# Self attention: projections of queries, keys and modulation without padding, spread to 32 rows a head through DRAM

## The chip, the cores and the metric

The kernel runs on one core of a Trainium2 chip. The core has five engines with their own instruction queues: TensorE (PE, matrix products into PSUM; its weight loads, PEld, overlap its products), VectorE (DVE), ScalarE (ACT), GpSimd (POOL) and SyncE (SP, which here issues most transfers between DRAM and the on-chip memory SBUF). Engines take their instructions in the order of their queues and wait for one another through semaphores. The transfers run on 16 DMA engines.

The metric is device time of one execution in microseconds (us), the median over runs. The profile is of one execution of its own; its times are made against that execution.

## The reference, cut to what matters

A post-norm decoder layer on 4 batches of 1,024 tokens and 256 features, all in 32-bit floats: self attention, cross attention with 154 context tokens, and a mixture of 8 experts, each followed by a layer norm. Only the first of the three concerns the change:

```python
q = (hidden_states @ Wq + bq).reshape(b, s, NH, HD).transpose(0, 2, 1, 3)
k = (hidden_states @ Wk + bk).reshape(b, s, NH, HD).transpose(0, 2, 1, 3)
v = (hidden_states @ Wv + bv).reshape(b, s, NH, HD).transpose(0, 2, 1, 3)
scores = jnp.einsum('bhqd,bhkd->bhqk', q, k) / jnp.sqrt(jnp.asarray(HD, q.dtype))
mod = jax.nn.sigmoid(hidden_states @ cg_W + cg_b + (cons_vec @ am_W + am_b))
scores = scores * mod.transpose(0, 2, 1)[..., None]
probs = jax.nn.softmax(scores, axis=-1)
ctx = jnp.einsum('bhqk,bhkd->bhqd', probs, v).transpose(0, 2, 1, 3).reshape(b, s, h)
causal_ctx = _mha(hidden_states, hidden_states, ca_Win, ca_bin, ca_Wout, ca_bout, CAUSAL_HEADS)
ctx = ctx * (1.0 - CAUSAL_W) + causal_ctx * CAUSAL_W
meta_ctx = _mha(ctx, ctx, mc_Win, mc_bin, mc_Wout, mc_bout, META_HEADS)
ctx = ctx * (1.0 - META_W) + meta_ctx * META_W
return ctx @ Wo + bo
```

There are NH = 16 heads of HD = 16 features. Each head and token has one modulation, a sigmoid, with which its scores are multiplied.

## The kernel before

**Layout of heads.** Queries and keys stand with features on the partitions and tokens along the row. A head has 16 features, but it is given 32 partitions, so that four heads (a group g of four, NG = 4) fill a tile of 128 partitions and each head lies on its own 32 rows of the PE array. Of the 32 rows, 16 are features, 15 are zero, and row 31 (MR) is special: in k it holds -1, in q it later takes the maximum of the token's scores. A product over all 32 rows is then the score less its maximum, which can go straight into the exponential.

The padding is made in the weights. load_head_cols (L141) loads a weight of 256 x 256 into a staging tile and copies its columns into a zeroed tile of 256 x 512, and load_head_bias (L153) does the same for a bias, with -1 in row 31 for k. cgw, the weight of the modulation, repeats each head's column 32 times.

**Projecting.** project (L283) multiplies 128 columns of such a weight with xT, the transposed tokens of the batch (256 x 1,024), into a PSUM tile "big" of 128 x 1,024; there are two of these tiles, shared with the score products. It is 4 products of 128 x 512, and each is two instructions in the profile, 8 in all. For each group there are three calls: project_mod (evacuated by ACT as a tanh, then scaled by POOL), project_q (evacuated by DVE, with the bias and the modulation) and project_k (evacuated by ACT with the bias). So a batch makes 12 calls. The tiles q and k come from a pool "qk" of 6, the modulation from a pool "ex" of 10.

**Maxima and exponentials.** For each group and each quarter (part) of 256 query tokens there are 8 units of each kind. A unit of maxima (L410) makes two score products (L422) into a "big" tile, and DVE takes the maximum over keys (L429); after 8 of them the maxima are transposed (L343) and added to row 31 of q (L346). A unit of exponentials (L441) makes the score products with all 32 rows (L460) and ACT exponentiates them (L471; L468 at the end of the batch); every four units a product with the values follows (L480).

**Order of a batch.** The loop over n (L829) runs 128 units of exponentials, 32 a group, with the maxima 12 units ahead (lead). In groups 0 to 2 it calls project_mod, project_q and project_k of the next group at units 4, 8 and 12 (project_at, L825). In group 3 it starts the causal attention instead. Then come two attentions of four heads each, the output product and the layer norm, the cross attention (L926 to L965), and, for the last norm of the batch, a generator that runs on into the next batch's loop ("behind").

begin(b) (L753) starts a batch: it transposes the tokens into xT, calls the three projections of group 0, makes the first 12 units of maxima and the values v16 and v64. For batch 0 it runs at once. For batches 1 to 3 it is a generator, and one step of it is taken at each step of the batch before, from its last output product on: two steps there, eight in the layer norm, and then one in each unit of the cross attention's loop, which has 36.

**Queues.** What an engine does is in the order of the program as the framework has placed it, and a wait in a queue holds all behind it. SP's queue at the start holds, in this order: the tokens of batch 0, the weights, the bias table and context of the cross attention, and a fill of the DRAM buffer scratch with zeros (L260, 9.2 MB in rows of 1 KB) and row numbers (L261, 9,216 pieces of 8 bytes), which the experts use at the end. After that SP issues four transfers a batch until the experts begin. POOL's queue at the start pads the weights and loads the biases.

Of the kernel before, what the change touches and what calls it, by code (L numbers as in the profile page):

```python
# [46 lines left out]
def decoder_layer(ctx: ExitStack, tc: tile.TileContext, a, out):  # L47
# [18 lines left out]
    def flat(t):  # L66
        return t.rearrange("p a b -> p (a b)")
# [65 lines left out]
    with tc.tile_pool(name="wA", bufs=1) as wA, tc.tile_pool(name="work", bufs=2) as work:  # L133


        def load_plain(name, src, n):
            t = wA.tile([P, src.shape[0] // P, n], F32, tag=name, name=name)
            nc.sync.dma_start(t, src.rearrange("(c p) n -> p c n", p=P))
            return t

        def load_head_cols(name, src):  # L141

            st = work.tile([P, NC2, H], F32, tag="ex", name="stage", bufs=EXB)
            nc.sync.dma_start(st, src.rearrange("(c p) n -> p c n", p=P))
# [8 lines left out]
        def load_head_bias(name, src, extra):  # L153

            t = wA.tile([P, NG], F32, tag=name, name=name)
            if extra == 0.0:
                nc.vector.memset(t, 0.0)
            else:
                tmp = work.tile([P, NG], F32, tag="tmpb", name="tmpb")
                nc.vector.memset(tmp, extra)  # L160
                nc.vector.tensor_scalar(t, tmp, rowmx, None, ALU.mult)
            v = src.rearrange("(g j d) -> j d g", j=4, d=HD)
            for j in range(4):
                nc.gpsimd.dma_start(t[32 * j : 32 * j + HD, :], v[j])
            return t

        def load_cols(name, src):
            t = wA.tile([P, src.shape[0] // P], F32, tag=name, name=name)
            nc.gpsimd.dma_start(t, src.rearrange("(c p) -> p c", p=P))
            return t  # L170
# [4 lines left out]
            return t  # L175


        idv = ident.rearrange("p (j w) -> p j w", w=32)
        rowmx = const.tile([P, 1], F32, name="rowmx")
        nc.vector.reduce_sum(rowmx, idv[:, :, MR], axis=AX.X)  # L180

        mxcol = []
        for i in range(2):
# [2 lines left out]
            mxcol.append(m)  # L186

        nc.sync.dma_start(gw, a["L0_ffn_gate_w"].rearrange("(c p) e -> p c e", p=P))
        wq = load_head_cols("wq", a["L0_attn_Wq"])
        bq = load_head_bias("bq", a["L0_attn_bq"], 0.0)  # L190

        cgs = work.tile([P, NC2, NH], F32, tag="cgs", name="cgs", bufs=1)
        nc.sync.dma_start(cgs, a["L0_attn_cg_W"].rearrange("(c p) h -> p c h", p=P))
        cgw = wA.tile([P, NC2, NH, 32], F32, tag="cgw", name="cgw")
        for c in range(NC2):
            nc.gpsimd.tensor_copy(cgw[:, c], cgs[:, c, :].unsqueeze(2).to_broadcast([P, NH, 32]))
# [5 lines left out]
        amr = work.tile([18, NH, 32], F32, tag="ex", name="amr", bufs=EXB)  # L202
        nc.vector.tensor_copy(amr, am.unsqueeze(2).to_broadcast([18, NH, 32]))
# [5 lines left out]
        cgb = wA.tile([P, NG], F32, tag="cgb", name="cgb")  # L209
        ps = small()  # L210
        for g in range(NG):
# [3 lines left out]
        nc.vector.tensor_scalar(cgb, ps[:, 0:NG], 0.5, None, ALU.mult)  # L215

        wk = load_head_cols("wk", a["L0_attn_Wk"])
        bk = load_head_bias("bk", a["L0_attn_bk"], -1.0)
        wv = load_plain("wv", a["L0_attn_Wv"], H)
        bv = load_bcast("bv", a["L0_attn_bv"])  # L220

# [17 lines left out]
        xbq = load_head_bias("xbq", a["L0_xattn_bq"], 0.0)  # L239
        xwk = load_head_cols("xwk", a["xWkT"])  # L240
        xbk = load_head_bias("xbk", a["L0_xattn_bk"], 0.0)
# [22 lines left out]
        def ex_tile(shape, name):  # L264
            return work.tile(shape, F32, tag="ex", name=name, bufs=EXB)
# [14 lines left out]
        def qk_tile(name):  # L280
            return work.tile([P, S], F32, tag="qk", name=name, bufs=6)

        def project(w, lo, xT):  # L283

            ps = big()
            for tb in range(2):
                for c in range(NC2):
                    nc.tensor.matmul(  # L288
                        ps[:, tb, :],
                        w[:, c, lo : lo + P],  # L290
                        xT[:, c, tb * 512 : (tb + 1) * 512],
                        start=(c == 0),
                        stop=(c == NC2 - 1),
                    )
            return ps
# [22 lines left out]
        class Clock:  # L318
# [62 lines left out]
        class Self:  # L381
# [4 lines left out]
                self.clock = Clock()  # L386
                self.st = [{} for _ in range(NG)]

            def project_mod(self, g):
                ms = project(cgw, g * P, self.xT)  # L390
                mod = ex_tile([P, S], "mod")
                nc.scalar.activation(
                    mod, flat(ms), AF.Tanh, bias=cgb[:, g : g + 1], scale=0.5
                )
                nc.gpsimd.tensor_scalar(mod, mod, 1.0, 0.5, ALU.add, ALU.mult)
                self.st[g]["mod"] = mod

            def project_q(self, g):
                q = self.st[g]["q"] = qk_tile("q")
                qs = project(wq, g * P, self.xT)  # L400
                nc.vector.scalar_tensor_tensor(
                    q, flat(qs), bq[:, g : g + 1], self.st[g]["mod"], ALU.add, ALU.mult
                )

            def project_k(self, g):
                k = self.st[g]["k"] = qk_tile("k")
                ks = project(wk, g * P, self.xT)
                nc.scalar.activation(k, flat(ks), AF.Identity, bias=bk[:, g : g + 1])

            def maxima(self, n):  # L410
                u, s = divmod(n, 8)
# [341 lines left out]
        def begin(b):  # L753

            y = ys[b]
            xT = work.tile([P, NC2, S], F32, tag="xT", name="xT", bufs=1)
            for c in range(NC2):
                transpose_tokens(xT, y, c)
                yield
            v16 = work.tile([P, NT, VP], F32, tag="v16", name="v16", bufs=1)  # L760
            nc.gpsimd.memset(v16, 1.0)
            sa = Self(xT, v16, None)
            for step in (sa.project_mod, sa.project_q, sa.project_k):
                step(0)
                yield
            add_bias(y, bo)
            v64 = work.tile([P, NT, H], F32, tag="v64", name="v64", bufs=1)
            begun[b] = sa, xT, v64
            vals = values(xT, wv, 0, bv, v16, NH, HD, 1)
            for n in range(lead):  # L770
                sa.maxima(n)
                next(vals, None)
                sa.clock.step()
                yield
            yield from values(xT, ca[0], 2 * H, ca[3], v64, MH, MD, 0)
# [36 lines left out]
        for b in range(B):  # L812
# [526 lines left out]
```

## Time and profile before

| What | Value |
|---|---|
| median of 3 runs | 3435.27 us (3431.95 to 3436.01) |
| the profiled execution | 3433.82 us |
| its span, first to last instruction | 3432.0 us |
| granted PE clock, mean | 0.976 |
| start, 0 to 80 us: PE busy, granted clock | 61.34 us, 0.74 |
| loop of batch 0, groups 0 to 2, 80 to 291 us: PE, DVE, ACT busy | 202.48, 130.87, 119.58 us |
| group 3 and the two attentions of four heads, 291 to 594 us: PE busy | 296.50 us |
| begin of batch 1 beside the layer norm, 594 to 620 us: PE, DVE busy | 26.00, 16.68 us |
| cross attention, 620 to 753 us: PE, DVE, ACT busy | 129.29, 73.01, 82.11 us |
| experts and end, 2773 to 3432 us: PE busy | 621.80 us |

A busy time is the time in which at least one instruction of that engine ran; matrix products overlap and their ends are modelled, so a busy PE need not be at its peak. A batch lasts 686 us: its context transfer is issued at 620.38, 1308.23 and 1994.39 us. In a line of the timeline the numbers are the start and the time taken; in a line of groups they are the number of instructions, the busy time, the mean of one in ns, and the engine's idle time before them with what ended it. PE here counts products and PEld weight loads.

### The profile page before, as it was taken

The page shows a single profiled execution, that of the slowest core. Times are in us where ns is not written, and L with a number is a line of the kernel's source. Part 1 is how long each engine was busy: PE and PEld are TensorE (multiplying, and loading weights), DVE is VectorE, ACT ScalarE, POOL GpSimd, SP SyncE. Part 2 cuts the span into 40 slices and gives each one's busy share as a digit, 9 for nine tenths or more (in the row PEclk, how much of TensorE's full clock was granted, in tenths as well). Part 3 has the DMA queues.
Part 4 walks back from the last instruction along what each step waited for, and adds up shares of the span by engine and source line. Part 5 has one row for each costly group of instructions (what it writes and reads, how often), then busy time and mean ns, then how long its engine had stood idle before and what let it go on. Part 6 is the DMA issues. An engine that isn't in the chain of part 4 may idle for free.

```text
span 3432.0 us, 60936 instructions
## 1 busy us (share of the span) xinstructions
PE 3300.5 (96%) x25260; PEld 2085.6 (61%) x25260; DVE 1725.3 (50%) x3571; ACT 1601.0 (47%) x3130; POOL 373.3 (11%) x601
## 2 busy tenths in 40 slices
PE   7999999999999999999999999999999999999997
PEld 4555667565556675665566756555667665555554
DVE  3565555565655555656555556565556551122224
ACT  1555534375555453755554537555534731222223
POOL 4000000000000000000000000000000018222123
PEclk7999999999999999999999999999999999999999
DMA  9000000000000000000000000000000052111114
GB/s 204 1 2 1 1 1 1 3 21 14 1 1 1 1 1 3 21 13 2 1 1 1 1 3 9 1 2 1 1 1 1 1 203 82 47 42 44 44 44 157
DMA packets 75866, 84.13 MB, mean 25 GB/s; under 512 B 15136, under 2 KB 65928, under 8 KB 75592
## 3 DMA queue, kind: packets, MB, share of 16 engines
q1 hardware_dynamic: 68040, 61.53, 6.4%
q0 software_dynamic: 7552, 18.70, 1.6%
q8 instruction: 202, 3.31, 0.4%
q14 instruction: 72, 0.59, 0.1%
HBM read 46.52 MB, written 33.69 MB: 23 GB/s over the span
## 4 chain that ended last, share of the span: by engine, by line
PE 85%; DVE 9%; ACT 2%; issue 2%; POOL 1%; DMA 1%; SPq 0%; ACTq 0%; DVEq 0%; POOLq 0%
PE big L288 10%; PE big L422 8%; PE big L530 8%; PE one L566 7%; PE acc L584 7%; PE big L1226 7%; PE one L480 7%; DVE mxp L429 6%; PE one L460 4%; PE acc L1248 4%; PE one L697 3%; PE big L1178 3%; PE big L662 3%; PE one L302 2%; PE acc L716 2%
## 5 line engine op out<-in xcount | busy, mean ns | idle before, releaser
L429 DVE TENSOR_REDUCE mxp<-big 128x2 f32<-128x1024 f32 x512 | 610.3, 1218 | 305.5 <-PE acc L460 252.1
L422 PE MATMUL big<-k,q 31*128 31x512 f32 x2048 | 595.8, 644 | 30.2 <-DVE mxp L429 26.6
L471 ACT ACTIVATE ex<-one 128x512 f32<-128x512 f32 x696 | 391.3, 601 | 247.4 <-PE acc L460 182.9
L460 PE MATMUL one<-q,k 32*128 32x256 f32 x2784 | 501.9, 397 | 0.0
L269 DVE CUSTOM_DVE_ANT_0 prob<-big,zero_t 128x1024 f32<-128x1024 f32 x256 | 303.6, 1222 | 271.9 <-PE big L530 271.7
L460 PEld LDWEIGHTS one<-q,k 32*128 32x128 f32 x2784 | 326.8, 186 | 31.0 <-ACT ex L471 2.5
L549 ACT ACTIVATE prob<-prob,nmx 128x1024 f32<-128x1024 f32 x256 | 293.0, 1153 | 20.2 <-DVE nmx L269 19.7
L530 PE MATMUL big<-mk,mq 64*128 64x512 f32 x1024 | 284.4, 633 | 2.5 <-ACT ex L468 2.5
L422 PEld LDWEIGHTS big<-k,q 31*128 31x128 f32 x2048 | 180.1, 189 | 171.5 <-DVE mxp L429 93.6
L571 ACT COPY pt<-one 128x512 f32<-128x512 f32 x256 | 137.8, 588 | 311.7 <-PE one L566 311.7
L566 PEld LDWEIGHTS one<-ident,prob 128*128 128x128 f32 x2048 | 221.8, 142 | 98.1 <-issue 92.4
L1226 PE MATMUL big<-wall,xt 128*128 x576 | 272.5, 596 | 1.8 <-POOL by L1202 1.8
L460 PE MATMUL acc<-q,k 32*128 32x256 f32 x928 | 263.9, 404 | 0.0
L566 PE MATMUL one<-ident,prob 128*128 128x128 f32 x2048 | 257.6, 279 | 0.0
L480 PE MATMUL one<-ex,v 128*32 128x256 f32 x4096 | 248.4, 382 | 0.0
L1236 DVE TENSOR_TENSOR hidr<-big,slr 128x512 f32<-128x512 f32 x72 | 49.8, 691 | 332.7 <-ACT slr L1234 332.7
L682 ACT ACTIVATE xs<-xs,xmx 128x154 f32<-128x154 f32 x512 | 174.4, 414 | 69.6 <-DVE xmx L269 69.6
L480 PEld LDWEIGHTS one<-ex,v 128*32 128x32 f32 x4096 | 119.8, 110 | 122.1 <-ACT ex L471 35.8
L573 DVE COPY pt<-one 128x512 f32<-128x512 f32 x256 | 164.3, 683 | 10.9 <-PE one L566 10.9
L269 DVE CUSTOM_DVE_ANT_0 xs<-big,bias 128x154 f32<-128x154 f32 x512 | 132.0, 314 | 66.0 <-ACT avx L724 33.5
L530 PEld LDWEIGHTS big<-mk,mq 64*128 64x128 f32 x1024 | 99.6, 191 | 101.7 <-issue 79.4
L460 PEld LDWEIGHTS acc<-q,k 32*128 32x128 f32 x928 | 155.4, 186 | 0.0
(266 smaller groups left out, 4715.2 us busy)
## 6 DMA issues: line engine op xcount, KB each, us to landing
xg<-scratch SPq DMA_DIRECT2D x72, 129.0 KB, 2.0
scratch<-empty SPq DMA_DIRECT2D x1, 9216.0 KB
r<-result SPq DMA_DIRECT2D x8, 1024.0 KB, 11.2
y<-in_x_dram SPq DMA_DIRECT2D x4, 1024.0 KB, 5.3
wall<-in_L_ffn_w_gate_dram SPq DMA_DIRECT2D x8, 512.0 KB, 10.3
wall<-in_L_ffn_w_up_dram SPq DMA_DIRECT2D x8, 512.0 KB, 10.8
wall<-in_L_ffn_w_down_dram SPq DMA_DIRECT2D x8, 512.0 KB, 11.6
bias<-in_fside_BxSxS_dram SPq DMA_DIRECT2D x4, 616.0 KB, 4.5
```

What stands on the lines that cost most here:

```text
L269: nc.vector.tensor_tensor_reduce(out=out, in0=ps, in1=bias, scale=-1.0, scalar=3.0e38, op0=ALU.add, op1=ALU.min, accum_out=low,)
L288: nc.tensor.matmul(ps[:, tb, :], w[:, c, lo : lo + P], xT[:, c, tb * 512 : (tb + 1) * 512], start=(c == 0), stop=(c == NC2 - 1),)
L422: nc.tensor.matmul(ps[:, jj, :], st["q"][r : r + MR, tok : tok + P], st["k"][r : r + MR, kb * 512 : (kb + 1) * 512], start=True, stop=True,)
L429: nc.vector.reduce_max(mxp[:, t, kb, 2 * pair : 2 * pair + 2], ps, axis=AX.X)
L460: nc.tensor.matmul(scs[jj][:, i * QW : (i + 1) * QW], st["k"][r : r + MR + 1, kc * P : (kc + 1) * P], st["q"][r : r + MR + 1, part * QW : ...
L471: nc.scalar.activation(ex[:, jj, :], scs[jj], AF.Exp, scale=1.0 / HD**0.5)
L480: nc.tensor.matmul(av[32 * j : 32 * j + 32, 0:QW], self.v[:, kc, h * VW : h * VW + 32], exs[kc // 2, j // 2][:, j % 2, i : i + QW], start= ...
L530: nc.tensor.matmul(pss[i][:, kb, :], q[r : r + MD, t * P : (t + 1) * P], k[r : r + MD, kb * 512 : (kb + 1) * 512], start=True, stop=True,)
L549: nc.scalar.activation(p, p, AF.Exp, bias=nmx[:, i : i + 1], scale=-1.0, accum_out=sm[:, t % 4, i : i + 1],)
L566: nc.tensor.transpose(ps[:, kc * P : (kc + 1) * P], probs[u][i][:, at : at + P], ident)
L584: nc.tensor.matmul(av[64 * i : 64 * i + 64, (t % 4) * P : (t % 4 + 1) * P], v[:, kc, h * MD : (h + 1) * MD], flipped[u][i][:, kc, :], star ...
L1226: nc.tensor.matmul(ps[:, g, :], xt[:, c * P : (c + 1) * P], wall[:, bass.ds(off + (g * NC2 + c) * D, D)], start=(c == 0), stop=(c == NC2 - 1),
```

## The change

The weights of queries, keys and modulation are no longer padded: wq and wk are loaded as they are (256 x 256), cgw repeats a head's column 16 times instead of 32, and the biases and cgb have 2 columns instead of 4. A projection of 128 columns now holds 8 heads, so all heads take two calls for each of the three (half 0 and half 1), 6 a batch instead of 12.

All six are made in begin. The evacuated tiles qh and kh hold 8 heads of 16 rows. Each is written to a DRAM buffer, q_rows or k_rows (512 rows of 1,024), with each head's 16 rows at the first 16 of its 32 (rows_of). The other 16 rows of each head are written once at the start from a tile pads: zeros for q, and zeros with -1 in the last row for k. A group's q and k are then loaded from 128 rows of these buffers (load): group 0's between the two halves in begin, the others' at unit 4 of the group before. All these transfers are issued by SP. Pads takes the place of xT in its pool of one tile. In begin three steps are added.

For padding, load_head_cols and load_head_bias stay in use for the cross attention alone. The scheduled order changes with it: at the start, SP's queue has the pads ahead of the weights, and the bias table and context behind the fill of scratch, where the writes and loads of batch 0's q and k follow.

```diff
+        pads = work.tile([P, 2, S], F32, tag="xT", name="pads", bufs=1)
+        nc.gpsimd.memset(pads[:, 0, :], 0.0)
+        idv = ident.rearrange("p (j w) -> p j w", w=HD)
+        last_of = const.tile([P, 1], F32, name="last_of")
+        nc.vector.reduce_sum(last_of, idv[:, :, HD - 1], axis=AX.X)
+        nc.vector.tensor_scalar(pads[:, 1, :], pads[:, 0, :], last_of, None, ALU.subtract)
+        qkd = [dram.tile([NG * P, S], F32, name=n) for n in ("q_rows", "k_rows")]
+
+        def rows_of(i, half, lo):
+
+            return qkd[i].rearrange("(t h w) s -> t h w s", t=NC2, w=32)[half, :, lo : lo + HD, :]
+
+        for i in range(2):
+            for half in range(NC2):
+                nc.sync.dma_start(rows_of(i, half, HD), pads[:, i, :])
...
-        wq = load_head_cols("wq", a["L0_attn_Wq"])
-        bq = load_head_bias("bq", a["L0_attn_bq"], 0.0)
+        wq = load_plain("wq", a["L0_attn_Wq"], H)
+        bq = load_cols("bq", a["L0_attn_bq"])
...
-        wk = load_head_cols("wk", a["L0_attn_Wk"])
-        bk = load_head_bias("bk", a["L0_attn_bk"], -1.0)
+        wk = load_plain("wk", a["L0_attn_Wk"], H)
+        bk = load_cols("bk", a["L0_attn_bk"])
...
-            def project_mod(self, g):
-                ms = project(cgw, g * P, self.xT)
+            def project(self, half):
+
+                ms = project(cgw, half * P, self.xT)
                 mod = ex_tile([P, S], "mod")
                 nc.scalar.activation(
-                    mod, flat(ms), AF.Tanh, bias=cgb[:, g : g + 1], scale=0.5
+                    mod, flat(ms), AF.Tanh, bias=cgb[:, half : half + 1], scale=0.5
                 )
                 nc.gpsimd.tensor_scalar(mod, mod, 1.0, 0.5, ALU.add, ALU.mult)
-                self.st[g]["mod"] = mod
-
-            def project_q(self, g):
-                q = self.st[g]["q"] = qk_tile("q")
-                qs = project(wq, g * P, self.xT)
+                yield
+                q = ex_tile([P, S], "qh")
+                qs = project(wq, half * P, self.xT)
                 nc.vector.scalar_tensor_tensor(
-                    q, flat(qs), bq[:, g : g + 1], self.st[g]["mod"], ALU.add, ALU.mult
+                    q, flat(qs), bq[:, half : half + 1], mod, ALU.add, ALU.mult
                 )
-
-            def project_k(self, g):
-                k = self.st[g]["k"] = qk_tile("k")
-                ks = project(wk, g * P, self.xT)
-                nc.scalar.activation(k, flat(ks), AF.Identity, bias=bk[:, g : g + 1])
+                nc.sync.dma_start(rows_of(0, half, 0), q)
+                yield
+                k = ex_tile([P, S], "kh")
+                ks = project(wk, half * P, self.xT)
+                nc.scalar.activation(k, flat(ks), AF.Identity, bias=bk[:, half : half + 1])
+                nc.sync.dma_start(rows_of(1, half, 0), k)
+                yield
+
+            def load(self, g):
+
+                for i, n in enumerate("qk"):
+                    t = self.st[g][n] = qk_tile(n)
+                    nc.sync.dma_start(t, qkd[i][g * P : (g + 1) * P, :])
...
-            for step in (sa.project_mod, sa.project_q, sa.project_k):
-                step(0)
-                yield
+            yield from sa.project(0)
+            sa.load(0)
+            yield from sa.project(1)
...
-            project_at = {4: sa.project_mod, 8: sa.project_q, 12: sa.project_k}
...
-                if g < 3 and s in project_at:
-                    project_at[s](g + 1)
+                if g < 3 and s == 4:
+                    sa.load(g + 1)
```

More of the change, by code (lines that the diff above doesn't have):

```diff
@@ L151, in load_head_cols, with load_head_bias @@
             return t.rearrange("p c h w -> p c (h w)")
-        def load_head_bias(name, src, extra):
+        def load_head_bias(name, src):
             t = wA.tile([P, NG], F32, tag=name, name=name)
[L156 to L161, printed above, removed]
+            nc.vector.memset(t, 0.0)
             v = src.rearrange("(g j d) -> j d g", j=4, d=HD)
@@ L175, in load_bcast @@
             return t
-        idv = ident.rearrange("p (j w) -> p j w", w=32)
-        rowmx = const.tile([P, 1], F32, name="rowmx")
-        nc.vector.reduce_sum(rowmx, idv[:, :, MR], axis=AX.X)
+        pads = work.tile([P, 2, S], F32, tag="xT", name="pads", bufs=1)
[10 more added lines that the diff above has]
+                nc.sync.dma_start(rows_of(i, half, HD), pads[:, i, :])
         mxcol = []
@@ L188, in decoder_layer @@
         nc.sync.dma_start(gw, a["L0_ffn_gate_w"].rearrange("(c p) e -> p c e", p=P))
-        wq = load_head_cols("wq", a["L0_attn_Wq"])
-        bq = load_head_bias("bq", a["L0_attn_bq"], 0.0)
+        wq = load_plain("wq", a["L0_attn_Wq"], H)
+        bq = load_cols("bq", a["L0_attn_bq"])
         cgs = work.tile([P, NC2, NH], F32, tag="cgs", name="cgs", bufs=1)
         nc.sync.dma_start(cgs, a["L0_attn_cg_W"].rearrange("(c p) h -> p c h", p=P))
-        cgw = wA.tile([P, NC2, NH, 32], F32, tag="cgw", name="cgw")
+        cgw = wA.tile([P, NC2, NH, HD], F32, tag="cgw", name="cgw")
         for c in range(NC2):
-            nc.gpsimd.tensor_copy(cgw[:, c], cgs[:, c, :].unsqueeze(2).to_broadcast([P, NH, 32]))
+            nc.gpsimd.tensor_copy(cgw[:, c], cgs[:, c, :].unsqueeze(2).to_broadcast([P, NH, HD]))
         cgw = cgw.rearrange("p c h w -> p c (h w)")
@@ L201, in decoder_layer @@
         nc.sync.dma_start(am[17:18, :], a["L0_attn_cg_b"].unsqueeze(0))
-        amr = work.tile([18, NH, 32], F32, tag="ex", name="amr", bufs=EXB)
-        nc.vector.tensor_copy(amr, am.unsqueeze(2).to_broadcast([18, NH, 32]))
+        amr = work.tile([18, NH, HD], F32, tag="ex", name="amr", bufs=EXB)
+        nc.vector.tensor_copy(amr, am.unsqueeze(2).to_broadcast([18, NH, HD]))
         amr = amr.rearrange("p h w -> p (h w)")
@@ L207, in decoder_layer @@
         nc.sync.dma_start(cons[0:16, :], a["L0_attn_cons_vec"].unsqueeze(1))
-        cgb = wA.tile([P, NG], F32, tag="cgb", name="cgb")
+        cgb = wA.tile([P, NC2], F32, tag="cgb", name="cgb")
         ps = small()
-        for g in range(NG):
+        for g in range(NC2):
             nc.tensor.matmul(
@@ L214, in decoder_layer @@
             )
-        nc.vector.tensor_scalar(cgb, ps[:, 0:NG], 0.5, None, ALU.mult)
-        wk = load_head_cols("wk", a["L0_attn_Wk"])
-        bk = load_head_bias("bk", a["L0_attn_bk"], -1.0)
+        nc.vector.tensor_scalar(cgb, ps[:, 0:NC2], 0.5, None, ALU.mult)
+        wk = load_plain("wk", a["L0_attn_Wk"], H)
+        bk = load_cols("bk", a["L0_attn_bk"])
         wv = load_plain("wv", a["L0_attn_Wv"], H)
@@ L238, in decoder_layer @@
         xwq = load_head_cols("xwq", a["xWqT"])
-        xbq = load_head_bias("xbq", a["L0_xattn_bq"], 0.0)
+        xbq = load_head_bias("xbq", a["L0_xattn_bq"])
         xwk = load_head_cols("xwk", a["xWkT"])
-        xbk = load_head_bias("xbk", a["L0_xattn_bk"], 0.0)
+        xbk = load_head_bias("xbk", a["L0_xattn_bk"])
         xwv = load_plain("xwv", a["xWvT"], H)
```

## The prediction

> **What bounds the kernel now.** I read the page's busy shares and chain first, then the loop stage by stage, then the start. Two lines of the page:
>
> ```profile
> PE 3300.5 (96%) x25260; PEld 2085.6 (61%) x25260; DVE 1725.3 (50%) x3571; ACT 1601.0 (47%) x3130; POOL 373.3 (11%) x601
> PE 85%; DVE 9%; ACT 2%; issue 2%; POOL 1%; DMA 1%; SPq 0%; ACTq 0%; DVEq 0%; POOLq 0%
> ```
>
> TensorE (PE) carries 85% of the chain that ends last, so an instruction taken off PE is worth time, unless the 9% of VectorE (DVE) takes over where it goes. The costs of the instructions concerned, in the groups by shape:
>
> ```profile
> L288 PE MATMUL big<-xT,cgw 128*128 128x512 f32 x128 | 59.9, 610 | 0.0
> L288 PE MATMUL big<-xT,wq 128*128 128x512 f32 x128 | 58.8, 602 | 2.1 <-DVE mxp L429 2.1
> L288 PE MATMUL big<-xT,wk 128*128 128x512 f32 x128 | 58.8, 602 | 0.0
> ```
>
> 128 = 4 batches x 4 groups x 8: one call of project is 8 instructions. They overlap; in the timeline their weight loads start 0.43 us apart (17.70, 18.13, 18.56 us), so a projection holds PE for 8 x 0.43 = 3.4 us. What it really costs in the loop is read from stretches. These four cover group 1 of batch 0, from the last exponential of group 0 to its own last: the first two together hold 16 units of the loop (the cut between them is arbitrary), each of the last two 8:
>
> ```profile
> 146.22:166.76 20.54, 19.86 (x179) 11.61 (x176) 11.53 (x14) 11.34 (x22) 1.77 (x2) 1.00 0.01 2
> 166.76:184.90 18.14, 17.65 (x178) 10.40 (x180) 10.43 (x13) 9.13 (x17) 0.72 (x1) 1.00 0.00 1
> 184.90:200.11 15.21, 14.47 (x168) 9.08 (x167) 10.23 (x14) 9.14 (x18) 0.72 (x1) 1.00 0.01 1
> 200.11:215.32 15.21, 14.48 (x168) 9.07 (x168) 10.23 (x14) 9.21 (x18) 0.72 (x1) 1.00 0.01 3
> ```
>
> The first number after the stretch is its length, then busy PE, weight loads, DVE, ACT, POOL. The three projections lie in the first two. Without them 8 units take 15.21 us, twice in a row: that is the pace when no projection is there, limits of DVE included. Three projections cost 20.54 + 18.14 - 2 x 15.21 = 8.26 us, a little less than their 10.3 us of PE.
>
> The start, from the timeline:
>
> ```profile
> 30.97 0.37 SPq L260 DMA_DIRECT2D scratch<-empty  x1
> 33.25 26.62 SPq L261 DMA_DIRECT2D scratch<-rows  x1
> 38.10 2.09 PE L422 MATMUL big<-k,q 31*128 31x512 f32 x8
> 41.50 3.21 PE L422 MATMUL big<-k,q 31*128 31x512 f32 x8 [1.31 <-DVE mxp L429]
> ...
> 68.99 3.35 PE L302 MATMUL one<-cawin,xT 128*128 128x256 f32 x7
> ```
>
> Batch 0's first maxima start at 38.10 us. Beside them SP issues the 9.2 MB fill of scratch and its 9,216 eight-byte pieces; its queue is held for 26.62 us, and the pieces land only 45.0 us after issue:
>
> ```profile
> scratch<-rows SPq DMA_DIRECT2D x1, 72.0 KB, 45.0
> ```
>
> That is at 78.25 us. Nobody waits for it now. This line decides the new kernel's start.
>
> [...] the eight-byte pieces run after the fill (289 GB/s in 31 to 63 us, then 31 GB/s to 78). [...] in the built program the loads of q and k do wait for the writes on SP. [...] the trace shows 0.50 in 38 to 69 us, after PE idled 9.2 us before L302.
>
> **The change part by part.**
>
> *Loop.* 9 projections a batch (groups 1 to 3) leave it, with their tanh, k and q evacuations on ACT and DVE. By the stretches, 8.26 us for each of 12 groups: 99.1 us. Bounds: 95 (some of the gap in a new place) to 12 x 10.3 = 123 (all of PE's time); in the first groups of batches 1 to 3 the end of the batch before is interleaved and more of the 10.3 may count. I take 100. The loads by groups, 8 of 512 KB a batch, lie in a stage where the DMA share is 0.01. By the order on SP those of groups 1 and 2 stand right after the next batch's begin, before anything of the loop, and wait for the cross attention's xq tiles; group 3's waits for group 0's tiles, which are free some 50 units (95 us) before they are used again. So they cost nothing; were a load late, each us would be a us of PE.
>
> *Begin of batches 1 to 3.* Half 1 adds three projections: 10.3 us of PE, beside work that fills PE (11.00 of 11 us busy in 609 to 620). Three pairs of maxima and values, 2.12 us each in this stage, move into the cross attention loop, where a unit grows by about as much: nothing, +-4. Now the round trip:
>
> ```profile
> 602.72 1.28 DVE L401 SCALAR_TENSOR_TENSOR q<-big,bq,mod 128x1024 f32<-128x1024 f32 x1 [1.82 <-PE big L288]
> 607.80 1.11 ACT L408 ACTIVATE k<-big,bk 128x1024 f32<-128x1024 f32 x1 [8.71 <-PE big L288]
> 609.41 1.13 PE L422 MATMUL big<-k,q 31*128 31x512 f32 x4
> ```
>
> kh of half 0 is ready at 608.9. [...] The load of 512 KB, by y (1,024 KB, 5.3 us) less half its data (1.5 us at some 340 GB/s; slices of the DMA view show 331 to 375 during the weights), takes 3.8: 617.4. The maxima now stand behind half 1's projections, at 609.4 + 10.3 = 619.7. The cover is 2.3 us; q is 5 us earlier. A longer trip stalls PE one for one, and everything on PE is behind it. Sum for three batches 31.5 us, bounds 22 and 45.
>
> *Start.* The built program's order on SP is: pads, weights, scratch<-empty, scratch<-rows, bias, cn, then the q and k rows of half 0 and q of half 1, then the loads of q and k. Everything of batch 0's attention queues behind the fill. [...] I take 94 for the first maxima, against 38.10.
>
> Not all is lost: the values of v16 and half 1 are done in the wait. Before, maxima and values at half clock take 38.10 to 68.99; maxima alone go two in 3.4 us (38.10 to 41.50), so 12 in 20.4, and 0.7 for transposes. The cawin values start at 94 + 21 = 115 instead of 69: 46 us later (bounds 38 and 57). [...] The POOL work that goes (the memsets and copies that pad wq and wk, eight small DMAs made two) lies under the fill: nothing.
>
> *Sum*, against the profiled execution (3433.82 us, its span 3432.0): 3433.8 - 100 + 31.5 + 46 = 3411.3. The median of the runs shown is 1.45 us above it: 3412.
>
> **Rivals.**
> - *The rows slip past the fill.* If the q and k rows don't wait for the eight-byte pieces (the 26.62 us of that issue end at 59.9, so SP itself is free from then), the maxima start near 70: 22 us instead of 46, 3389. For it: few bytes are left by then[...].
> - *No gain.* The wait at the start is longer, first maxima at 115, or each begin costs 18 us instead of 10.5: about 3434. [...] Against: it takes a miss of 21 us in all.
> - *Slower.* The start alone eats everything. [...] price: one us of span per us of delay. It decides from first maxima at 125 us on, because (125 - 48) + 31.5 - 100 = +8.5. At 130 us, 3449. For it: PE has nothing else to do then. [...]
>
> **How the numbers follow.** About 0.2% (6.9 us: from 3428.4 to 3442.1) is what a measurement of this kernel can tell from no change. Forecast 0.79 (3396 to 3428), slip past 0.08, no gain 0.08, slower 0.05. Faster 0.87, same 0.08, slower 0.05. The range 3394 to 3429 takes the bounds of loop, begin and start, not all at one end, and a part of the first rival.
>
> **What would show it.** First maxima near 94 us, after q and k landed, PE idle before them some 40 us; units of 15.21 us per 8 through groups 0 to 2, 60.8 us a group instead of 69.1; maxima of batch 1 with no wait for a DMA; the begin-to-loop stretch some 10 us longer. Wrong: a DMA named before the maxima of batches 1 to 3 or of a later group, first maxima far from 94 us, or a pace of 8 units that is not 15.2 because DVE's maxima, now undisturbed, run into ACT or PSUM instead.

## The result, and the profile after

| | Before | After |
|---|---|---|
| median | 3435.64 us | 3402.19 us (3400.24 to 3405.18) |
| profiled execution, span | 3432.0 us | 3403.1 us |
| granted PE clock, mean | 0.976 | 0.977 |

The ratio is 0.991, 95% interval 0.9895 to 0.9922: 33 us faster, where 23 were forecast. The time lies inside the range.

The page of the kernel after, its busy shares and the chain that ended last, by engine:

```profile
PE 3221.1 (95%) x25064; PEld 2044.0 (60%) x25064; DVE 1718.1 (50%) x3561; ACT 1584.7 (47%) x3114; POOL 359.1 (11%) x582
PE 76%; DVE 11%; DMA 4%; issue 4%; POOL 3%; ACT 2%; SPq 1%; ACTq 0%; DVEq 0%; POOLq 0%
```

PE works 79 us less, and its share of the chain falls from 85% to 76%. DMA, POOL, DVE and issue each have 2 to 3 points more; a part of that is the new start, below. The groups by shape show the 6 projections a batch that are left (64 = 4 batches x 2 halves x 8):

```profile
L296 PE MATMUL big<-xT,cgw 128*128 128x512 f32 x64 | 31.3, 631 | 0.0
L296 PE MATMUL big<-xT,wq 128*128 128x512 f32 x64 | 28.8, 592 | 0.0
L296 PE MATMUL big<-xT,wk 128*128 128x512 f32 x64 | 28.8, 592 | 0.0
```

**The loop.** Group 1 of batch 0 in four stretches of 8 units (from the busy times by stretch; after the length come PE, PEld, DVE, ACT, POOL, then the granted clock, the DMA share and GB/s):

```profile
188.91:204.13 15.22, 14.49 (x168) 9.08 (x168) 10.24 (x14) 9.15 (x19) 0.73 (x1) 1.00 0.20 69
204.13:219.35 15.22, 14.49 (x168) 9.08 (x168) 10.24 (x14) 9.15 (x19) 0.73 (x1) 1.00 0.00 1
219.35:234.57 15.22, 14.49 (x168) 9.08 (x168) 10.24 (x14) 9.15 (x18) 0.73 (x1) 1.00 0.00 1
234.57:249.78 15.21, 14.47 (x168) 9.07 (x167) 10.23 (x14) 9.14 (x18) 0.72 (x1) 1.00 0.01 2
```

All four have the pace that only the last two had before. The group takes 60.87 us instead of 69.10. The first stretch carries a load of rows (DMA share 0.20) and is no longer than the others.

**The start.** SP's queue, from the timeline (start, time taken):

```profile
34.52 30.41 SPq L269 DMA_DIRECT2D scratch<-rows  x1
64.98 17.38 SPq L831 DMA_DIRECT2D bias<-in_fside_BxSxS_dram  x1
...
83.06 0.59 SPq L411 DMA_DIRECT2D q_rows<-qh  x1
83.75 0.59 SPq L416 DMA_DIRECT2D k_rows<-kh  x1
84.43 1.20 SPq L411 DMA_DIRECT2D q_rows<-qh  x1
90.85 0.36 SPq L423 DMA_DIRECT2D q<-q_rows  x1
93.35 0.34 SPq L423 DMA_DIRECT2D k<-k_rows  x1
```

The 9,216 small pieces hold SP for 30.41 us, and the next issue, a table that nobody needs yet, for 17.38 more. Only then do the rows of batch 0 leave. PE, from the same view:

```profile
98.24 2.09 PE L437 MATMUL big<-k,q 31*128 31x512 f32 x8 [39.59 <-DMA k<-k_rows]
...
119.88 0.79 PE L310 MATMUL one<-cawin,xT 128*128 128x256 f32 x1
```

PE stood idle for 39.59 us until k had landed. The cawin values start at 119.88 us instead of 68.99.

**The beginning of a batch.** SP and then PE, in batch 1's:

```profile
627.50 0.58 SPq L411 DMA_DIRECT2D q_rows<-qh  x1
633.50 0.32 SPq L423 DMA_DIRECT2D q<-q_rows  x1
633.92 0.59 SPq L416 DMA_DIRECT2D k_rows<-kh  x1
640.39 0.32 SPq L423 DMA_DIRECT2D k<-k_rows  x1
```

```profile
639.66 3.60 PE L296 MATMUL big<-xT,wk 128*128 128x512 f32 x8
643.67 1.13 PE L437 MATMUL big<-k,q 31*128 31x512 f32 x4 [0.42 <-DMA k<-k_rows]
```

ScalarE had kh ready at 632.37 us, but SP was held at the load of q, which waits for the write of q. So the write of k went out 1.5 us late, and its receipt took 6.5 us (640.39 - 633.92). The maxima waited 0.42 us: half 1's projections cover the round trip, and nothing is left over.

**Where the 28.9 us come from.** The spans cut at the ends of exponentials (the first and last of each group; the first and last unit of the cross attention's loop):

| Stage | Before | After | Difference |
|---|---|---|---|
| start to the first unit | 80.31 | 131.23 | +50.9 |
| groups 0 to 2 of batch 0 | 204.1 | 179.4 | -24.7 |
| groups 1 and 2 of batches 1 to 3 | 414.6 | 365.2 | -49.4 |
| group 0 of batches 1 to 3 | 240.6 | 232.4 | -8.2 |
| group 3, four batches | 322.5 | 315.7 | -6.8 |
| group 3 to the cross loop, batches 0 to 2 | 813.5 | 822.3 | +8.7 |
| cross loop, batches 0 to 2, and on to the next first unit | 349.4 | 349.2 | -0.3 |
| the rest | | | +0.9 |

Two lines do not fit the forecast: group 0 of the later batches gains a third of what the other groups gain, and the cross loop, which takes over moved maxima, grows by nothing. In both the granted clock changes. The stretches of batch 0 from group 3 to the cross loop, its cross loop, and group 0 of batch 1, first before, then after:

```profile
365.03:636.22 271.19, 267.57 (x2117) 180.64 (x2117) 151.01 (x276) 122.68 (x217) 21.91 (x29) 1.00 0.01 2
636.22:739.91 103.69, 103.34 (x816) 67.14 (x816) 61.75 (x303) 66.20 (x182) 0.00 (x0) 0.94 0.01 1
753.25:834.07 80.82, 78.00 (x721) 49.76 (x724) 50.53 (x77) 42.49 (x76) 3.22 (x4) 0.96 0.09 27
```

```profile
388.52:662.52 274.00, 271.33 (x2114) 182.04 (x2114) 146.87 (x263) 124.97 (x218) 23.19 (x30) 1.00 0.04 13
662.52:765.69 103.17, 102.48 (x845) 66.52 (x842) 67.29 (x316) 66.74 (x182) 0.00 (x0) 1.00 0.06 20
779.01:857.52 78.51, 74.72 (x696) 47.66 (x698) 48.07 (x75) 40.11 (x75) 2.18 (x3) 0.89 0.09 28
```

The clock of the cross loop rises from 0.94 to 1.00, that of group 0 falls from 0.96 to 0.89. The clock records give 13.5 us at half clock in the cross loop before and none after, and in group 0 6.8 us before and 17.1 after. The experiments had to settle what belongs to the work and what to the clock.

### The profile page after: what moved, and what is told of

It reads as the page before. It is cut to its first block, busy times and chain, and to the rows that moved or that the text cites. A ratio compares the mean times of both kernels' runs of the same rounds, so it can differ in the third digit from the quotient of the medians.

```text
span 3403.1 us, 60618 instructions
## 1 busy us (share of the span) xinstructions
PE 3221.1 (95%) x25064; PEld 2044.0 (60%) x25064; DVE 1718.1 (50%) x3561; ACT 1584.7 (47%) x3114; POOL 359.1 (11%) x582
## 4 chain that ended last, share of the span: by engine, by line
PE 76%; DVE 11%; DMA 4%; issue 4%; POOL 3%; ACT 2%; SPq 1%; ACTq 0%; DVEq 0%; POOLq 0%
PE big L437 8%; PE big L545 7%; PE one L581 7%; DVE mxp L444 7%; PE acc L599 7%; PE big L1240 7%; PE one L495 7%; PE big L296 6%; PE acc L1262 4%; PE one L475 4%; PE one L712 3%; PE big L677 2%; PE one L310 2%; PE acc L731 2%; PE big L645 2%
## 5 line engine op out<-in xcount | busy, mean ns | idle before, releaser
L437 PE MATMUL big<-k,q 31*128 31x512 f32 x2048 | 616.8, 643 | 71.3 <-DMA k<-k_rows 41.1
L437 PEld LDWEIGHTS big<-k,q 31*128 31x128 f32 x2048 | 187.1, 189 | 217.2 <-DVE mxp L444 95.6
L495 PE MATMUL one<-ex,v 128*32 128x256 f32 x4096 | 255.7, 391 | 5.0 <-DVE q L354 5.0
L508 POOL TENSOR_TENSOR avq<-avq 128x256 f32<-128x256 f32 x64 | 46.4, 726 | 1108.2 <-ACT avq L503 1108.2
```

The source lines that it names most:

```text
L437: nc.tensor.matmul(ps[:, jj, :], st["q"][r : r + MR, tok : tok + P], st["k"][r : r + MR, kb * 512 : (kb + 1) * 512], start=True, stop=True,)
L495: nc.tensor.matmul(av[32 * j : 32 * j + 32, 0:QW], self.v[:, kc, h * VW : h * VW + 32], exs[kc // 2, j // 2][:, j % 2, i : i + QW], start= ...
```

## The experiments

In all of them "rows" are the writes and loads of q_rows and k_rows, and "first maxima" the start of the first L437 of batch 0. Ratios are against the kernel before. A difference in us is one of medians; the kernel before, run beside each experiment, had medians from 3431.71 to 3435.87 us, so a few us between two experiments are not sure.

**1. The same kernel once more (after_again)**, for what differs between two executions of one program.

> The changed kernel as it is, a second time. [...] the lengths of group 3 of a batch differ between executions: 77.9 us without such a stretch, about 80.6 with 6.8 us of it, about 82 with 10.2 us of it, and which batch has it changes. If the lengths are set by the program's order alone (rival), batch 2 is again the one with 82.0 and the others have 77.9. The total is within 0.2% of 3402 in both.

Measured: 3401.86 us, ratio 0.9907 (0.9891 to 0.9924). All four groups 3 took 77.9 us, where that of batch 2 had taken 82.00 with 10.2 us at half clock: so such a stretch is not set by the order of the program alone. Group 0 of batches 1 to 3 took 75.25, 75.32 and 73.71 us with 10.2, 10.2 and 6.8 us at half clock; in the first execution 78.50, 76.96 and 76.92 with 17.1, 13.7 and 13.7. Groups 1 and 2 agree within 0.03 us. So group 0 varies with its clock alone. All kernels below that leave group 0 as it is fall on one line: 72.6 us at 3.4, 73.7 to 74.3 at 6.8, 75.2 to 75.3 at 10.2, 76.9 at 13.7, 78.5 at 17.1. That is (78.5 - 72.6) / 13.7 = 0.43 us for each us at half clock. The cross loop has about the same price: that of batch 2 took 108.97 us here with 13.7 us at half clock and 103.01 in the first execution without, 0.44 us for each.

**2. The fill out of the way (fill_late)**: the two scratch transfers, and the POOL work that makes their sources, are tied to group 2's q of batch 0, so they go out when no rows wait.

```diff
-        nc.sync.dma_start(sv[:, :, 0:H], empty.unsqueeze(1).to_broadcast([P, TILES, H]))
-        nc.sync.dma_start(sv[:, :, H:RW], rows)
...
+                if b == 0 and n == 70:
+                    fill_scratch(sa.st[g]["q"])
```

> The changed kernel with the fill of scratch made from a product of group 2's q with zero, so that its two transfers are issued in batch 0's group 2 instead of at the start. If batch 0's start waits for the fill alone (theory), the first maxima come when PE has done the values and projections, at 57 to 62 us instead of 98.2, and the total falls by about 38 us to 3364. If the round trip through DRAM or POOL's work at the start sets it (rival), the first maxima stay after 88 us and the total falls by less than 10.

Measured: 3366.74 us, ratio 0.9805 (0.9789 to 0.9821): 35 us under the changed kernel. The first maxima on PE's timeline, and group 2 of batch 0, which now carries most of the fill (its issue starts at 208.87 us, in the last 6 us of group 1):

```profile
55.51 1.71 PE L441 MATMUL big<-k,q 31*128 31x512 f32 x8 [0.63 <-DMA k<-k_rows]
```

```profile
214.60:275.47 60.87, 57.94 (x660) 36.29 (x660) 40.95 (x50) 36.57 (x72) 2.90 (x4) 1.00 0.80 131
```

The first maxima are 43 us earlier, a little ahead of the theory's 57 to 62, and the time is within 3 us of its 3364. The fill keeps the DMA engines busy at 0.80 there and costs the loop nothing: 60.87 us, as without it, and group 1 takes 60.87 too. Most of the start's loss is the fill ahead of the rows.

**3. The same for the kernel before (before_fill_late)**: does the fill cost the old order anything?

> The kernel before with the same late fill. If nobody waited for the fill there (theory), its first maxima stay at 38 us and the total within 0.2% of 3435. If its traffic slowed the loads and biases of the start there too (rival), it is 5 to 15 us faster.

Measured: 3430.84 us, ratio 0.9989 (0.998 to 0.9998). The first maxima start at 37.28 us instead of 38.10, and the first unit ends at 77.71 us instead of 80.31, with 3.4 us less at half clock. The median is 5.0 us lower, inside the theory's 0.2% and at the lower edge of the rival. So the fill costs 35 us with the change and 4 to 5 without (under 7 by the interval). It is not a defect of the old kernel that the new one inherited; the rows made a wait out of a transfer that nobody had waited for.

**4. Dense products given back to group 0 (dummy_dense)**: three projections that nobody reads, at units 4, 8 and 12 of group 0 of batches 1 to 3. The results are not changed by them.

```diff
+                if b > 0 and g == 0 and s in (4, 8, 12):
+                    project(wq, 0, xT)
```

> The changed kernel with three projections that nobody reads put back into group 0 of batches 1 to 3, at units 4, 8 and 12, as before: 3 x 3 x 8 dense products more, no evacuation. Clock theory: these dense products kept PE at full clock there; group 0 grows by at most 4 us from 76.9 to 78.5, its half-clock time falls from 10 to 17 us to 7 or less, the total by 5 to 12 us at most to 3407 to 3414. Rival, plain work: each costs the 2.75 us that it costs in groups 1 and 2, group 0 becomes 85 to 87 us, the total 3427.

Measured: 3417.7 us, ratio 0.995 (0.9934 to 0.9967): 15.5 us over the changed kernel, between the two theories. Group 0 of batch 1:

```profile
779.74:858.93 79.19, 76.37 (x719) 48.23 (x722) 48.18 (x75) 40.26 (x74) 2.17 (x3) 0.98 0.09 28
```

Both are at work. Half clock falls to 3.4, 6.8 and 6.8 us in the three groups. At equal half clock (6.8 us) a group 0 takes 80.8 to 80.9 us with the three projections and 73.7 to 74.3 without: they cost some 7 us. In the profiled execution of the change 4 to 5 of these come back as lower clock, but it had the most half clock of all. The 21 groups 0 without dense projections (seven kernels) have 10.1 us of it on average, the 12 with them (four kernels) 5.5: at 0.43 some 2 us come back, and 3 x (7 - 2) is the 15 that was measured.

The traces show where. The products with the values in the changed kernel, as a group of the page and at one place of group 0 of batch 1:

```profile
L495 PE MATMUL one<-ex,v 128*32 128x256 f32 x4096 | 255.7, 391 | 5.0 <-DVE q L354 5.0
792.40 3.32 PE L495 MATMUL one<-ex,v 128*32 128x256 f32 x32 [1.68 <-DVE q L354]
```

PE waits 1.68 us for the maxima that DVE adds into q, because DVE has the layer norm of the batch before in front of them; it is so in each of the three groups (5.0 us in all). Where projections stand in group 0 (before, and experiments 3, 4 and 6), this wait is 0.0: they covered it, which fits a group 0 that gives 7 us and not 8.23. Half clock starts right behind the wait, at 792.8 us here, in 11 of the 21 groups 0 without projections and in 0 of the 12 with them. A second stretch starts in all 33, 2 to 5 us after the start of the 32 products with the gate's weight (gw, 8 columns), and lasts 3.4 to 6.8 us with projections and 3.4 to 13.7 without.

**5. The half of the beginning, doubled (dummy_begin)**: three more projections that nobody reads, after half 1's, in the beginnings of batches 1 to 3.

```diff
             yield from sa.project(1)
+            if b > 0:
+                for _ in range(3):
+                    project(wq, 0, xT)
+                    yield
```

> What the beginning of a batch pays for three more dense projections: the changed kernel with three projections that nobody reads, after those of the second half, in the beginnings of batches 1 to 3 (24 more products of 128 columns each time; no evacuation, no transfer, no table). This doubles the suspected cost by itself. Theory 'the full price, with the clock apart' (the prediction's step, 10.3 us a batch, was right in kind, and only a lower clock before the change hid it): +8 to +11 us a batch in the stretch from the end of the fourth group to the first unit of the causal sublayer or the one that follows, so 3426 to 3435 us. Rival 'the beginning has room' (what the stages measured, 2.8 us a batch, is the price): +2 to +4 us a batch, 3408 to 3414 us. Second rival 'they come as cover': they lie in the round trip's shadow and cost nothing, 3400 to 3405 us.

Measured: 3430.73 us, ratio 0.999 (0.9983 to 0.9997): 28.5 us more. The same stretches as above:

```profile
387.14:663.28 276.14, 273.30 (x2103) 182.40 (x2104) 142.71 (x257) 124.97 (x218) 23.16 (x30) 1.00 0.04 13
663.28:776.56 113.28, 112.40 (x878) 71.07 (x877) 71.25 (x321) 66.77 (x183) 0.00 (x0) 1.00 0.06 18
789.88:863.58 73.70, 69.85 (x696) 46.02 (x698) 48.06 (x75) 40.05 (x74) 2.17 (x3) 0.95 0.10 30
```

At the same clock (1.00 in both) they lengthen the way to the cross loop by 2.1 us and the cross loop by 10.1: 12.2 us a batch, a little over the theory's 8 to 11. Three times that is 36.6, less what group 0 gains in clock (73.70 instead of 78.50 here). The beginning has no room; more dense work in it pays its full price. The rival, that 2.8 us a batch is the price, falls, and so does the one that they come as cover.

**6. Half 1 out of the beginning (half1_in_loop)**: its three projections go to units 4, 8 and 12 of group 0 of batches 1 to 3.

```diff
-            yield from sa.project(1)
+            if b == 0:
+                yield from sa.project(1)
...
+                if b > 0 and g == 0 and s in (4, 8, 12):
+                    if s == 4:
+                        late = sa.project(1)
+                    next(late)
```

> The second half's three projections of batches 1 to 3 leave the beginning and go to units 4, 8 and 12 of the loop's group 0 (that half's rows are read from group 2 on). Theory 'the second half's projections cover the round trip': the beginning loses 8 to 10 us of work, but TensorE then waits 8 to 10 us for the rows of the first half before the first maxima, nothing gained there; group 0 becomes 4 to 7 us longer (as three unread projections at those units did): 3409 to 3420 us. Rival 'the round trip was not near': the beginning gets 8 to 10 us shorter without a wait before the first maxima, and group 0 pays for it 5 us: 3385 to 3397 us.

Measured: 3434.6 us, ratio 1.0013 (0.9999 to 1.0027): 32 us over the changed kernel, above even the first theory. PE's timeline in the beginning of batch 1, and the stretches up to and through the cross loop:

```profile
628.64 4.48 PE L310 MATMUL one<-wv,xT 128*128 128x256 f32 x20
639.71 2.09 PE L437 MATMUL big<-k,q 31*128 31x512 f32 x8 [6.59 <-DMA k<-k_rows]
```

```profile
384.37:666.15 281.78, 270.94 (x2114) 183.60 (x2114) 150.04 (x268) 122.75 (x216) 21.92 (x29) 0.97 0.03 9
666.15:764.02 97.87, 97.44 (x821) 64.29 (x818) 63.03 (x310) 66.46 (x183) 0.00 (x0) 1.00 0.04 12
```

Without half 1's projections in front, PE waits 6.59 us for the rows of half 0, even though the framework moved values into the gap. The wait does more than its length: the clock records show half clock for 17.1 us from 638.1 us on, and in the beginnings of batches 2 and 3 it is 17.1 us again. So with 10 us of work less in the beginning the way to the cross loop is 7.8 us longer, and only the cross loop gets 5.3 us shorter (0.6 in batches 1 and 2, which have 10.2 us at half clock in it); the three first groups that take the work are 10.8 us longer together. The theory's mechanism holds, with a wait a little under its 8 to 10 us; its price was too low, because it counted the wait and not the clock after it. The second stretch gives a size that was wanted: a cross loop at full clock with one half's work in the beginning takes 97.87 us, against 103.17 with two.

**7. The pads behind the weights as well (fill_pads_late)**: fill_late, and the pads' four writes after the weights wq, wk and wv (pads also leaves the pool of xT).

> The late scratch fill as in fill_late, and the pads' four row writes behind the weights of the self attention instead of ahead of them on SP. Theory 'the start is bound by SP's order and the queues, piece by piece': the first weights land earlier and the first maxima come 5 to 12 us ahead of the 55.5 us in fill_late, 43 to 50 us; 3353 to 3362 us. Rival 'what remains is the round trip and the modulation's biases from POOL': the first maxima stay at 53 to 56 us and the time at 3364 to 3368 us.

Measured: 3361.74 us, ratio 0.9788 (0.9772 to 0.9805), a time of the theory's, but the first maxima start at 55.73 us: the rival is right. The first unit ends 3.4 us earlier than in fill_late, and that goes with the clock (41.0 instead of 47.8 us at half clock up to there); nothing of the difference is an earlier start. What held the rows, on DVE's timeline and POOL's:

```profile
34.96 0.15 DVE L259 TENSOR_SCALAR nds<-nds 128x1 f32<-128x1 f32 x1 [8.18 <-DMA nds<-in_ds_dram]
...
41.38 1.27 DVE L413 SCALAR_TENSOR_TENSOR qh<-big,bq,mod 128x1024 f32<-128x1024 f32 x1
```

```profile
37.59 1.04 POOL L409 TENSOR_SCALAR mod<-mod 128x1024 f32<-128x1024 f32 x1
```

ACT had made the tanh by 18.5 us, but POOL, in order, came to it at 37.59, and DVE, in order, stood before a scalar for the cross attention until 34.96.

**8. These two queues cleared (start_dve)**: the small biases' scales go from DVE to POOL; of batch 0, the values' memset and the modulation's second step go from POOL to DVE.

> fill_pads_late, with what stood ahead of the first rows of batch 0 on POOL and VectorE taken off: the scales of three small biases go from VectorE to POOL (where the transfers that they wait for are issued), and of batch 0 the values' memset and the modulation's second step go from POOL to VectorE. Theory 'an in-order engine's queue held the first query rows back': in fill_pads_late the q_rows write was issued at 42.68 us because VectorE had waited to 34.96 us for the bias nds and POOL reached the modulation only at 37.59 us; SP is free of the weights at 36.4 us, so the write is issued at 36 to 37 us and the first maxima start 6 us earlier, at 48 to 51 us: 3353 to 3358 us. Rival 'the start is bound by what SP still issues and by the queues': first maxima at 54 to 56 us, 3360 to 3364 us.

Measured: 3353.72 us, ratio 0.9774 (0.9756 to 0.9792). SP's timeline:

```profile
36.61 0.59 SPq L416 DMA_DIRECT2D q_rows<-qh  x1
37.30 1.28 SPq L421 DMA_DIRECT2D k_rows<-kh  x1
45.17 0.35 SPq L428 DMA_DIRECT2D q<-q_rows  x1
47.62 0.34 SPq L428 DMA_DIRECT2D k<-k_rows  x1
```

The write goes out 6 us earlier, as expected, but with k's write beside it its receipt now takes 8.6 us. The first maxima come at 51.97 us, 1 us later than the theory's upper end; the time fits, but the interval overlaps that of fill_pads_late.

**9. The rows of batch 0 on ScalarE's queue (start_act)**, so that they do not stand behind SP's weights.

> start_dve, and the row writes of batch 0 and the loads of its first group go out from ScalarE's queue instead of SP's, so that they don't stand behind SP's weights. Theory 'SP's order is the last thing ahead of the rows': q_rows written at 26 to 30 us, first maxima at 40 to 46 us, 3344 to 3353 us. Rival [...]: the writes take 10 us or more instead of 6.5, first maxima at 47 to 51 us, no change from start_dve.

Measured: 3358.29 us, ratio 0.978 (0.9764 to 0.9796): no gain, first maxima at 52.38 us. ACT's timeline:

```profile
33.94 1.15 ACTq L416 DMA_DIRECT2D q_rows<-qh  x1
35.19 1.11 ACT L420 ACTIVATE kh<-big,bk 128x1024 f32<-128x1024 f32 x1 [16.61 <-DMA q_rows<-qh]
36.34 0.59 ACTq L421 DMA_DIRECT2D k_rows<-kh  x1
42.45 0.36 ACTq L428 DMA_DIRECT2D q<-q_rows  x1
```

qh was ready at 30.3 us, yet the issue came at 33.94, only 2.7 us ahead of SP's in start_dve. From write to load it took 8.5 us. ScalarE itself was held by the issue: kh waited for it. The theory's first maxima at 40 to 46 us did not come. The rival's end is met, its longer write only in part: 8.5 us and not 10. What held the issue, the transfers in front of it or a wait for the pads' writes, was not tried.

The version that beats both kernels is start_dve: 0.9774, 46 to 48 us below the changed kernel (by ratios and by medians). It keeps the whole change.

## Why the prediction was right, and where it was not

**Loop: right in mechanism and pace, one group in four mis-sized.** The pace of 15.21 us for 8 units held everywhere, the loads by groups cost nothing, and 8.23 us a group came out of groups 0 to 2 of batch 0 and groups 1 and 2 of the others: 74.1 us of 9 groups. The term took the same for the first groups of batches 1 to 3 and noted only that they might save more. They saved 8.2 us in all, and 16.4 in the second execution of the same program, whose cross loop of batch 2 took 6.0 more. Experiment 4 has the reason: at equal clock a first group saves some 7 us, with PE then waiting 1.68 us behind DVE's layer norm; and a part of that is given back, more or less by chance of the execution, because the first groups without dense products had more time at half clock (10.1 us on average, 5.5 with them). The step took the projections' price from a group without such work beside it.

**Beginnings: the price was near, its base was not.** The term was 31.5 us; the stages show +8.7 and -0.3, so 8.5. Experiment 5 rules out that the work is cheap there: at equal clock three projections cost 12.2 us, some 2 more than their 10.3 us of PE, with no evacuation and no transfer. The three pairs of maxima and values that move on were put at nothing; they may be the rest, which was not tried alone. What the sum missed is that the kernel before ran 10.2 to 13.5 us of each cross loop at half clock, which at 0.43 us each makes 4.4 to 5.8 us a batch. Corrected for it, a cross loop of before takes 103.69 - 13.5 x 0.43 = 97.9 us, the same as the 97.87 of experiment 6. So the change costs 2.8 + 5.3 = 8.1 us a batch at equal clock, 24 in all, inside the bounds of 22 and 45, and some 15 were paid back by the clock, which the forecast had no term for. Why the three of experiment 5 cost 4 us a batch more than these is open.

That the second half's products are what lifts the clock is supported by a count: of the cross loops of batches 0 to 2, 8 of 9 show more than 10 us at half clock in the three kernels with three projections in the beginning of a later batch (before and experiments 3 and 6), and 1 of 24 in the eight kernels with six or more. Short waits may have a part in it: in the 3.4 us in front of the three stretches of before PE is busy for 2.04, 2.81 and 2.76 us, at the same place in the changed kernel for 3.05 to 3.13. But the one cross loop of after_again that fell did so after 3.05 too, and dummy_begin has 2.47 us just ahead of its cross loops and keeps its clock, so they alone don't decide. Which property of the work the clock follows was not tried.

**The round trip: the cover of 2.3 us was used up.** The write took 6.0 and 6.5 us, where 4.4 was the author's estimate (the time to landing of kept<-y's 1,024 KB before), and k's was issued 1.5 us late behind q's load on SP; the load took about 3 us instead of 3.8. The wait came to 0.42 us, and to 0.77 and 0.34 in batches 2 and 3. A DMA named in front of these maxima was one of the forecast's own signs of being wrong; it was wrong by under 1 us each time. The step's claim that a longer trip stalls PE one for one was too mild: experiment 6 shows 17.1 us at half clock with a wait of 6.59.

**Start: right, 5 us short.** The forecast had first maxima at 94 us, the author's estimate, and the cawin values at 115; they came at 98.24 and 119.88, 50.9 us later than before instead of 46. The order of the queue was as read: q_rows' write at 83.06 us stands behind the pieces. It was SP that was held, for 17.38 us more at the bias table, and little but the pieces moved until then (4 GB/s from 73 to 82 us). The first rival's point that SP is free once the issue of the pieces has ended did not hold. Whether rows issued earlier would have had to wait for the pieces, the trace doesn't show. From 88 to 91 us, with rows being written, 210 GB/s moved at a DMA share of 0.51 (share and GB/s are the last two columns), less than the 331 to 375 that the prediction read during the weights:

```profile
88.00:91.00 3.00, 0.00 (x0) 0.00 (x0) 0.86 (x1) 2.48 (x2) 0.00 (x0) 0.50 0.51 210
```

**The sum.** Loop 18 us short of the forecast (82.4 of 100), beginnings 23 us better, group 3 with 6.8 us that were not forecast, start 5 us and the rest 1 us worse: of the span 28.9 us go where 22.5 were forecast, by errors that mostly cancel: that the sum came so near is in part luck. The other 3 us or so between 3412 and 3402 lie between the profiled executions and the medians. Group 3's gain is clock too: 77.9 us without half clock, 80.6 with 6.8 us of it. The kernel before shows 6.8 us in all four group 3; of the changed kernels' 36 groups 14 show half clock, so a part of it is chance.

**The rivals.** Rows that slip past the fill did not occur (98.24 us, not 70). No gain and slower would have needed 115 and 125 us.

## What to carry to other kernels

A transfer that nobody waits for is harmless only where it stands: before a new wait is put behind it on a queue, move it, since here a fill of 9.2 MB with 9,216 small pieces behind it cost 4 to 5 us in the old order and 35 in the new. A round trip through DRAM wants independent dense work laid over it, about 10 us for 0.5 MB here (6.5 us from the write of k_rows to the load, 3.3 more to the first maxima), and a gap there can cost more than its length: with the 6.59 us of experiment 6 came 17.1 us at half clock. When dense products are taken out of a stage, read the granted clock of that stage and its neighbours in both kernels before a saving is booked: a part can be paid back, or paid out, in clock, as in the cross loop (0.94 before, 1.00 after) and in group 0 (0.96 and 0.89). And look for the waits that the products had covered, here 1.68 us: they come out when the products go.

## What the runs showed of the hardware

- A us at half clock cost 0.43 us in the loop's group 0, in all kernels here that leave this group as it is, and 0.44 in the cross loop (experiment 1). The stretches come in steps of 3.4 us (3.4, 6.8, 10.2, 13.7, 17.1).
- At the start of the kernel before, half clock began at 31.9 us, within the 9.21 us in which PE stood idle, and lasted 41.0 us. Other drops came with PE at work. In the 3.4 us in front of the one in the cross loop of batch 0 before (636.0 us), PE was busy for 2.04; in front of the one in group 0 of batch 1 (786.2 us), for 3.29, mostly with the gate's products of 8 columns. Such a drop came within 2 to 5 us of the start of these products in 33 of 33 groups 0; that they cause it was not tried. Once down, PE ran 13.5 us of the cross loop at half clock, though it is recorded busy for 103.34 of its 103.69 us. From 1.6 us before the end of a wait of 6.59 us on, half clock lasted 17.1 us (experiment 6).
- A transfer of 9,216 pieces of 8 bytes held the issuing queue for 26.62 us before and 30.41 after, where the issue right behind it on that queue was held for 17.38 us more.
- A fill of 9.2 MB beside the loop, at a DMA share of 0.80, left group 2 at 60.87 us, to the hundredth what it takes without it.
